# Two layers of attention-like convolution on one core: products moved to GpSimd, a bias product and a DMA moved, one stage of image 0 nested

## The chip, the cores and the metric

The kernel runs on one core of a Trainium2 chip. The core has TensorE (PE, matrix products, with its own row PEld for loading weights), VectorE (DVE), ScalarE (ACT), GpSimd (POOL) and SyncE (SP, here only a queue that issues DMAs). ScalarE and GpSimd issue DMAs too. The metric is the device time of one execution in microseconds, as the median over the runs.

## The reference

The input is 8 images of 512 channels and 32 x 32 = 1024 positions, all in float32. Layer 0 is attention with 8 heads of 64 channels, a projection and a residual; layer 1 is a product of two 1x1 convolutions without softmax, followed by a normalization over the whole batch.

```python
# layer 0
q, k, v = conv1x1(x, Wq, bq), conv1x1(x, Wk, bk), conv1x1(x, Wv, bv)   # as (B, 8, 64, 1024)
attn = softmax(einsum('bhdn,bhdm->bhnm', q, k) * 64 ** -0.5, axis=-1)
x = x + conv1x1(einsum('bhnm,bhdm->bhdn', attn, v), Wp, bp)
# layer 1
g, theta, phi = conv1x1(x, g_w, g_b), conv1x1(x, theta_w, theta_b), conv1x1(x, phi_w, phi_b)  # 256 channels
f = einsum('bcn,bdn->bcd', theta, phi) / 1024
z = conv1x1(einsum('bcd,bdn->bcn', f, g), W_w, W_b) + x
out = (z - mean(z)) * rsqrt(var(z) + 1e-5) * gamma + beta      # mean and var per channel over batch and positions
```

## The kernel before, in words

The images run one after the other. For each, PE works through stages: attention (scores, exponential on ScalarE, weighted sum of v), then the q, v and k of the *next* image, then the projection of the current image (`project`), theta and phi (`theta_phi`), g, the 256 x 256 product f, and z. Image 0's q, k and v come first of all, in the order q, k, v, and attention follows them directly; for later images the order is q, v, k, and the projection follows.

Large products are done by a Strassen-like scheme of seven smaller products instead of eight (`seven`). Some of the seven can be split once more in the same way (`nested`). The table `INNER` says which: with three of them nested, four remain plain (`FOUR`). Nesting needs sums of blocks of the data (`inner_sums`, `inner_parts`) and of the weights, both made on VectorE. The weights' sums are made once, in place, in `keep_inner`, and the result is copied to memory and reloaded for each later image. In the kernel before, image 0's q, k and v use seven plain products, since the inner sums of the weights aren't there yet, and `keep_inner` runs after each stage.

The products of a stage go to banks of PSUM, and the parts are read by ScalarE (the first contribution to an output block) and by VectorE (those added to it). A bank is used again when its readers are done. Banks have tags, and a list `free` passes them from stage to stage; `seven` reorders it at the end. Attention takes its first three score tiles from the first, second and fourth tag of that list.

The denominators of the softmax are sums over keys of the exponentials. VectorE adds the exponentials (`acc`, L456 and L458), and the accumulating DMAs from GpSimd's queue fold them (`together`, L488). For images 0 to 6, `all_denominators` (L518) is called inside the next image's q stage: 16 matmul records sum the folds, VectorE takes the reciprocal (L524), a DMA from ScalarE's queue writes it to memory (L526), and four DMAs from SyncE's queue read it back into a tile `r`, broadcast over the partitions (L569). Four products (L555, in `normalize`) then multiply the attention's output `o` by `r`. They are called at units 7, 8, 10 and 11 of the next image's v stage. The sums `t_o` over `o` for the projection are made during the k stage. In image 0, `bias_product` (L189) also runs there, after the denominators: it multiplies Wp by v's bias, so that the bias can be added after the projection; its weights were prepared during attention (`join_bias`).

The last image has no next image to fill its wait. Its denominators come in two halves (`denominators`, L532). The first is done during attention. The second is done during the g stage of image 6: reciprocal (L537), a DMA of 16 x 256 values from SyncE's queue (L541), and two broadcasts of 512 KB each (L550) for each half. The last four products and the projection follow.

The order on VectorE, PE and parts of SyncE's queue is the order of the program where an instruction is passed to `dve`, `pe` or `sp`. Otherwise a scheduler chooses it. The dictionaries `fills` hang small pieces of work behind numbered units of a stage. A unit is about one PSUM part of a product.

Of the kernel before, what the change touches and what calls it, by code (L numbers as in the profile page):

```python
# [8 lines left out]
F32 = mybir.dt.float32  # L9
I32 = mybir.dt.int32  # L10
AF = mybir.ActivationFunctionType
ALU = mybir.AluOpType
# [4 lines left out]
P = 128  # L17
# [13 lines left out]
def unshifted(ctx: ExitStack, tc: tile.TileContext, a: dict, out: bass.AP):  # L31
    nc = tc.nc
    B, C, H, W = a["x"].shape
    N = H * W
    CC = C // P
# [127 lines left out]
    def keep_inner(name, w):  # L163

        for n in range(len(INNER[name])):
            a11, a12, a22, a21, s2, s3, s4 = inner_blocks(w, name, n)
            for to, l, r, op in ((s3, a11, a21, ALU.subtract), (a21, a21, a22, ALU.add), (s2, a21, a11, ALU.subtract),
                                 (s4, a12, s2, ALU.subtract)):
                dve(nc.vector.tensor_tensor(to, l, r, op))
        wide = len(INNER[name]) * 3 * P  # L170
        kept[name] = dram.tile([P, 14 * w.shape[3] + wide], F32, tag=f"kept_{name}", name=f"kept_{name}")
        nc.sync.dma_start(kept[name][:, :14 * w.shape[3]], w.rearrange("p i k f -> p (i k f)"))
        nc.sync.dma_start(kept[name][:, 14 * w.shape[3]:], rest[name][:, :wide])
# [15 lines left out]
    def bias_product(t, ps):  # L189
        for oc in range(CC):  # L190
            pe(nc.tensor.matmul(ps[:, oc:oc + 1], t[:, oc * P:(oc + 1) * P], ones, start=True, stop=True,
                                skip_group_check=True))
        nc.vector.tensor_tensor(bp, bp, ps, ALU.add)
# [229 lines left out]
    def attention(b, q, k, v, near_end, make_f=None):  # L423
# [94 lines left out]
        def all_denominators(ps):  # L518

            t = folded.pop("t")  # L520
            den = ps[:, 0, :256]
# [6 lines left out]
            if b == 0:  # L528
                bias_product(t[:, 3, :], ps[:, 1, :CC])
            return d.rearrange("(j k x) m -> j k (x m)", j=2, k=2)  # L530

        def denominators(g, ps):  # L532
# [8 lines left out]
            nc.sync.dma_start(d, ri.rearrange("(x s) n -> x s n", s=8)[:, 0, :])  # L541
# [10 lines left out]
        def normalize(d):  # L552

            def product(at, of):
                dve(nc.vector.tensor_tensor(at, at, of, ALU.mult))  # L555
# [289 lines left out]
    data = {"11": b11, "21": b21, "22": b22, "t1": t[0], "t2": t[1], "t3": t[2], "t4": t[3]}  # L845
# [9 lines left out]
    k = heads_of(0, "k", w, bk, data, dve)  # L855
    keep_inner("WkT", w)
    load_w(nc.sync)
    w = weights("WvT")
    v = values(0, w, data)
    keep_inner("WvT", w)  # L860
    load_w(nc.sync)
    held = {}
    for b in range(B):
# [23 lines left out]
        if not last:  # L887
# [20 lines left out]
            else:  # L908
                w_p = loaded[1][1]
                for unit, which in ((12, (3, 4)), (14, (5, 6))):  # L910
                    fills[unit] = lambda which=which: weight_sums(w_p, corner["WpT"], which, dve)
# [277 lines left out]
```

## Time and profile before

| what | value |
|---|---|
| median of 3 runs | 2139.47 us (2138.54 to 2140.98) |
| the profiled execution, its own time | 2139.02 us |
| its span, first to last instruction | 2137.2 us |
| PE busy | 2111.9 us, 12982 matmul records |
| VectorE busy | 1411.3 us |
| ScalarE busy | 745.8 us |
| GpSimd busy | 144.9 us (189 DMA issues of 766 ns) |
| mean granted clock of PE | 0.995 |
| one image in the middle (attention to attention) | 261.5 us |

One float32 matmul appears as several records: a product of 128 x 128 weights with 512 columns takes 0.43 us of PE and shows as two. Records overlap: the mean duration in a group (593 ns for such a record) is longer than the distance between two starts. PE is busy nearly all the time, so the places where it waits matter, and with them the clock it is granted.

In lines of the timeline the first number is the start in us from the beginning of the span and the second the duration. Behind the engine come the line of the program, the operation and "output<-inputs". Square brackets hold idle time of the engine before it and what ended it. In a table of stretches each engine has its busy time and, in brackets, its number of instructions; the columns are length, PE, PEld, DVE, ACT, POOL, the granted clock (1.00 is full), the share of DMA time and GB/s.

### The profile page before, as it was taken

To read this page: it belongs to the slowest core of one execution; us is meant where nothing else is said; L and a number is where in the kernel's file an instruction comes from. 1 tells how busy PE (TensorE), PEld (TensorE's weight loads), DVE (VectorE), ACT (ScalarE), POOL (GpSimd) and SP (SyncE) were. 2 spreads that over 40 slices of the span, in tenths; PEclk is the share of its full clock that TensorE was granted. 3 is DMA by queue.
4 is the path that set the end of the run, shared out by engine and by line. 5 is a ranking of instruction groups with operands and counts; after the bars stand their busy time and mean duration, and the time that the engine had idled before them with its cause. 6 is when DMAs were issued, how large, how long until landed. Compare 5 with 4: busy or idle time off the path is not lost.

```text
span 2137.2 us, 31130 instructions
## 1 busy us (share of the span) xinstructions
PE 2111.9 (99%) x12982; PEld 1127.2 (53%) x12982; DVE 1411.3 (66%) x1855; ACT 745.8 (35%) x869; POOL 144.9 (7%) x193
## 2 busy tenths in 40 slices
PE   9999999999999999999999999999999999999996
PEld 4534764347733567335673366633766347643462
DVE  5466667676576675766757677676774676656746
ACT  1464103641046310463105631066212652056106
POOL 0011000110001100010001100011000110011000
PEclk9999999999999999999999999999999999999998
DMA  6522444225142241423324242242334224122758
GB/s 208 192 41 35 121 192 136 41 30 163 73 140 40 43 146 73 145 39 60 125 94 127 40 99 86 114 107 41 99 133 173 38 38 131 56 56 40 224 201 343
DMA packets 53318, 228.75 MB, mean 107 GB/s; under 512 B 10673, under 2 KB 17329, under 8 KB 45617
## 3 DMA queue, kind: packets, MB, share of 16 engines
q1 hardware_dynamic: 42272, 200.34, 27.2%
q0 software_dynamic: 9072, 24.78, 9.6%
q8 instruction: 104, 1.70, 0.3%
q10 hardware_dynamic: 1824, 1.55, 0.3%
q14 instruction: 46, 0.37, 0.1%
HBM read 146.23 MB, written 46.86 MB: 90 GB/s over the span
## 4 chain that ended last, share of the span: by engine, by line
PE 97%; ACT 1%; DVE 1%; DMA 1%; issue 0%; SPq 0%; DVEq 0%; ACTq 0%
PE ps L449 21%; PE po L475 21%; PE ptp L310 9%; PE pp L310 7%; PE pq L310 6%; PE pv L310 6%; PE pk L310 5%; PE pg L310 4%; PE pv_in_s L258 3%; PE pq_in_s L261 3%; PE pk_in_s L261 3%; PE pz L310 3%; PE pf L657 2%; PE pp_in_s L261 2%; PE pwf L712 1%; ACT z L832 1%
## 5 line engine op out<-in xcount | busy, mean ns | idle before, releaser
L452 ACT ACTIVATE e<-ps 128x1024 f32<-128x1024 f32 x512 | 522.3, 1023 | 429.1 <-PE ps L449 422.9
L458 DVE TENSOR_TENSOR acc<-acc,e 128x1024 f32<-128x1024 f32 x384 | 470.2, 1225 | 143.4 <-ACT e L452 140.0
L449 PE MATMUL ps<-q,k 64*64 64x512 f32 x4096 | 529.8, 590 | 0.0
L475 PE MATMUL po<-e,v 64*64 64x512 f32 x4096 | 529.0, 589 | 0.0
L475 PEld LDWEIGHTS po<-e,v 64*64 64x64 f32 x4096 | 156.7, 133 | 282.8 <-issue 275.3
L449 PEld LDWEIGHTS ps<-q,k 64*64 64x64 f32 x4096 | 155.4, 133 | 283.5 <-issue 274.5
L488 POOL DMA_DIRECT2D fold<-acc x189 | 144.7, 766 | 1837.3 <-PE ps L449 746.5
L700 ACT ACTIVATE g<-pg,gb 128x512 f32<-128x512 f32 x31 | 21.3, 687 | 476.4 <-PE pg L310 476.3
L456 DVE TENSOR_TENSOR acc<-e,e 128x1024 f32<-128x1024 f32 x64 | 78.4, 1225 | 133.9 <-ACT e L452 133.9
L310 PE MATMUL ptp<-w_tp,t_x 128*128 128x256 f32 x512 | 114.4, 380 | 0.0
L310 PEld LDWEIGHTS ptp<-w_tp,t_x 128*128 128x128 f32 x512 | 97.5, 190 | 13.0
L310 PE MATMUL pp<-t_o,w_WpT 128*128 128x512 f32 x208 | 100.9, 593 | 0.0
L310 PE MATMUL pv<-w_WvT,t_x 128*128 128x256 f32 x400 | 100.8, 380 | 0.0
L310 PE MATMUL pq<-t_x,w_WqT 128*128 128x512 f32 x200 | 100.6, 596 | 0.0
L310 PE MATMUL pk<-t_x,w_WkT 128*128 128x512 f32 x200 | 100.1, 593 | 0.0
L310 PE MATMUL ptp<-w_tp,x 128*128 128x256 f32 x384 | 86.8, 380 | 0.0
L420 DVE TENSOR_TENSOR v<-v,pv_in_s 128x256 f32<-128x256 f32 x119 | 49.8, 421 | 56.0 <-PE pv_in_s L258 39.5
L336 DVE TENSOR_TENSOR k<-k,pk_in_s 128x256 f32<-128x256 f32 x119 | 47.9, 420 | 48.9 <-PE pk_in_s L261 36.5
L310 PEld LDWEIGHTS ptp<-w_tp,x 128*128 128x128 f32 x384 | 73.1, 190 | 13.2 <-issue 3.8
L336 DVE TENSOR_TENSOR q<-q,pq_in_s 128x256 f32<-128x256 f32 x119 | 48.2, 417 | 46.4 <-PE pq_in_s L261 34.1
L310 PEld LDWEIGHTS pv<-w_WvT,t_x 128*128 128x128 f32 x400 | 69.7, 191 | 5.9
L310 PE MATMUL pp<-o,w_WpT 128*128 128x512 f32 x144 | 67.8, 593 | 1.9 <-DVE o L555 1.9
(198 smaller groups left out, 2305.6 us busy)
## 6 DMA issues: line engine op xcount, KB each, us to landing
fold<-acc POOLq DMA_DIRECT2D x189, 128.0 KB, 3.1
w_WqT<-kept_WqT SPq DMA_DIRECT2D x7, 2368.0 KB, 8.8
w_WvT<-kept_WvT SPq DMA_DIRECT2D x7, 2368.0 KB, 8.5
w_WkT<-kept_WkT SPq DMA_DIRECT2D x7, 2368.0 KB, 16.2
r<-den_d SPq DMA_DIRECT2D x32, 512.0 KB, 6.9
x<-in_x_dram SPq DMA_DIRECT2D x30, 512.0 KB, 5.9
w_WpT<-kept_WpT SPq DMA_DIRECT2D x6, 2176.0 KB, 8.2
w_tp<-kept_tp SPq DMA_DIRECT2D x7, 1792.0 KB, 7.4
```

The lines of the kernel that those rows point to most:

```text
L258: pe(nc.tensor.matmul(ps[:, i, :], d[di][:, i * P:(i + 1) * P], a[wi], start=s not in begun and not i, stop=True, skip_group_check=True))
L261: pe(nc.tensor.matmul(ps, a[wi], d[di], start=s not in begun, stop=True, skip_group_check=True))
L310: pe(nc.tensor.matmul(to_ps, lhsT(k), rhs(k), start=(s, at) not in begun, stop=(k == nk - 1), skip_group_check=True))
L336: pin(nc.vector.tensor_tensor(at, at, ps if len(ps.shape) == 3 else ps.unsqueeze(1), ALU.add))
L420: lambda q, ps: dve(nc.vector.tensor_tensor(at(q), at(q), as_v(ps), ALU.add)), **how)
L449: pe(nc.tensor.matmul(ps[c * P // 2:(c + 1) * P // 2, j, :], k[r, p, keys], q[r, p, h * 512:(h + 1) * 512], start=True, stop=True, skip_gr ...
L452: nc.scalar.activation(e, ps, AF.Exp, scale=SCALE)
L456: nc.vector.tensor_tensor(accs[u], es[u, 0], e, ALU.add)
L458: ins = nc.vector.tensor_tensor(accs[u], accs[u], e, ALU.add)
L475: pe(nc.tensor.matmul(ps[j * D:(j + 1) * D, r, :], v[keys, m, (2 * p + j) * D:(2 * p + j + 1) * D], e[keys, j, :], start=(m == 0), stop=(m ...
L488: nc.gpsimd.dma_start(to, part_of, accum_op=ALU.add)
L657: pe(nc.tensor.matmul(to, theta[l][:, i, :], phi[r][:, i, :], start=(i == 0), stop=(i == NB // 2 - 1), skip_group_check=True))
```

## The change

Five edits:

- The four products of `o` with `r` are issued on GpSimd instead of VectorE for images 0 to 6. The last image keeps VectorE.
- In image 0 `bias_product` comes before the matmuls of the denominators instead of after the reciprocal. Its result is copied out of PSUM by ScalarE first, and VectorE adds the copy.
- The last DMA of reciprocals (second half, last image) is issued from ScalarE's queue instead of SyncE's.
- Image 0's v uses the nested scheme with three nested products. For that the inner sums of the data are made in image 0's k stage, the inner sums of Wv before the v stage, and those of Wk during it, in three parts. The copies of the weights to memory change places accordingly.
- In image 0 the four sums for Wp are made one by one at units 8, 9, 12 and 13 of the k stage instead of two each at 12 and 14.

```diff
     def keep_inner(name, w):
         for n in range(len(INNER[name])):
-            a11, a12, a22, a21, s2, s3, s4 = inner_blocks(w, name, n)
-            for to, l, r, op in ((s3, a11, a21, ALU.subtract), (a21, a21, a22, ALU.add), (s2, a21, a11, ALU.subtract),
-                                 (s4, a12, s2, ALU.subtract)):
-                dve(nc.vector.tensor_tensor(to, l, r, op))
+            inner_weights(name, w, n)
+        keep_all(name, w)
+
+    def inner_weights(name, w, n):
+        a11, a12, a22, a21, s2, s3, s4 = inner_blocks(w, name, n)
+        for to, l, r, op in ((s3, a11, a21, ALU.subtract), (a21, a21, a22, ALU.add), (s2, a21, a11, ALU.subtract),
+                             (s4, a12, s2, ALU.subtract)):
+            dve(nc.vector.tensor_tensor(to, l, r, op))
+
+    def keep_all(name, w):
...
@@ bias_product
-        nc.vector.tensor_tensor(bp, bp, ps, ALU.add)
+        got = small.tile([P, CC], F32, tag="got", name="got")
+        nc.scalar.copy(got, ps)
+        nc.vector.tensor_tensor(bp, bp, got, ALU.add)
@@ all_denominators
             t = folded.pop("t")
+            if b == 0:
+                bias_product(t[:, 3, :], ps[:, 1, :CC])
             den = ps[:, 0, :256]
...
-            if b == 0:
-                bias_product(t[:, 3, :], ps[:, 1, :CC])
@@ denominators
-            nc.sync.dma_start(d, ri.rearrange("(x s) n -> x s n", s=8)[:, 0, :])
+            (nc.scalar if g else nc.sync).dma_start(d, ri.rearrange("(x s) n -> x s n", s=8)[:, 0, :])
@@ normalize
             def product(at, of):
-                dve(nc.vector.tensor_tensor(at, at, of, ALU.mult))
+                if make_f:
+                    dve(nc.vector.tensor_tensor(at, at, of, ALU.mult))
+                else:
+                    dve(nc.gpsimd.tensor_tensor(at, at, of, ALU.mult))
@@ image 0
-    data = {"11": b11, "21": b21, "22": b22, "t1": t[0], "t2": t[1], "t3": t[2], "t4": t[3]}
+    data = {"11": b11, "21": b21, "22": b22, "t1": t[0], "t2": t[1], "t3": t[2], "t4": t[3], "name": "x_0"}
...
-    k = heads_of(0, "k", w, bk, data, dve)
-    keep_inner("WkT", w)
+    k = heads_of(0, "k", w, bk, data, dve,
+                 fills={unit: lambda of=of: inner_sums(data, of, dve) for unit, of in ((8, "21"), (10, "22"), (12, "t4"))})
+    wk, w = w, weights("WvT")
+    keep_inner("WvT", w)
+    v = values(0, w, data, inner="WvT",
+               fills={unit: lambda n=n: inner_weights("WkT", wk, n) for n, unit in enumerate((9, 11, 13))})
+    keep_all("WkT", wk)
     load_w(nc.sync)
-    w = weights("WvT")
-    v = values(0, w, data)
-    keep_inner("WvT", w)
     load_w(nc.sync)
@@ fills of the next image's k, image 0 only
-                for unit, which in ((12, (3, 4)), (14, (5, 6))):
-                    fills[unit] = lambda which=which: weight_sums(w_p, corner["WpT"], which, dve)
+                for unit, which in ((8, 3), (9, 4), (12, 5), (13, 6)):
+                    fills[unit] = lambda which=which: weight_sums(w_p, corner["WpT"], (which,), dve)
```

`nc.gpsimd.tensor_tensor` is the same operation as on VectorE, and `nc.scalar.dma_start` the same DMA from another queue.

## The prediction

> **What bounds the kernel now.** I read the page's busy table first (TensorE, PE, busy 2111.9 of 2137.2 us, VectorE only 1411.3), then the waits of PE, then a table of stages. PE's busy time can hide a slow clock, so I also asked for the granted clock. The waits of PE alone; columns are microseconds in total, times, longest:
>
> ```profile
> PE den L191 <- DVE fold L524: 1.9, 1, 1.9
> PE pp L310 <- DVE o L555: 1.9, 1, 1.9
> PE warm_ps L357 <- DVE folds L367: 1.1, 1, 1.1
> PE pk_in_s L261 <- DVE k L336: 0.3, 1, 0.3
> ```
>
> That is all: four waits in 12982 matmuls. The other images run without a gap, so work taken off another engine there gains nothing. The stages (start:end, length, PE busy):
>
> ```profile
> 53.80:78.04 24.24, 24.24 (x113) 21.12 (x111) 6.68 (x15) 4.30 (x5) 0.00 (x0) 1.00 0.50 201
> 209.78:215.04 5.26, 3.38 (x29) 2.18 (x29) 2.34 (x3) 0.00 (x0) 0.00 (x0) 1.00 0.03 9
> 215.04:239.90 24.86, 24.86 (x149) 22.75 (x148) 15.05 (x24) 4.53 (x7) 0.00 (x0) 0.93 0.64 185
> 239.90:263.30 23.40, 23.07 (x76) 14.01 (x75) 16.17 (x27) 5.64 (x10) 0.00 (x0) 1.00 0.18 51
> 741.10:764.29 23.19, 23.19 (x150) 21.56 (x149) 15.37 (x25) 4.53 (x7) 0.00 (x0) 1.00 0.69 199
> 764.29:787.15 22.86, 22.86 (x77) 14.01 (x76) 15.67 (x28) 5.64 (x10) 0.00 (x0) 1.00 0.26 98
> ...
> 216.00:217.00 1.00, 1.00 (x4) 0.82 (x3) 1.00 (x2) 0.00 (x0) 0.00 (x0) 0.50 0.00 0
> ```
>
> Line 1 is image 0's v with seven plain products; line 5 is a later image's v, with nested products, 1.05 us shorter. Line 2 is the denominators and bias product of image 0, with 1.88 us in which PE stood still. Line 3 is the v stage behind them: the same work as line 5 but 1.67 us longer, because the clock (third number from the right) fell to half, as the last line shows. Lines 4 and 6 are the k stages: image 0 loses 0.5.
>
> The end of the last attention and the order on VectorE (DVE) inside a later image, from the timeline (start, duration) and the table of DMA issues (KB each, us to landing):
>
> ```profile
> 1997.81 0.51 SPq L541 DMA_DIRECT2D den_d<-ri  x1
> 2003.49 1.09 SPq L550 DMA_DIRECT2D r<-den_d  x2
> 2010.41 2.36 DVE L555 TENSOR_TENSOR o<-o,r 128x1024 f32<-128x1024 f32 x2 [3.38 <-DMA r<-den_d]
> den_d<-ri SPq DMA_DIRECT2D x1, 16.0 KB, 5.7
> den_d<-fold ACTq DMA_DIRECT2D x1, 32.0 KB, 1.7
> 759.18 1.22 DVE L555 TENSOR_TENSOR o<-o,r 128x1024 f32<-128x1024 f32 x1
> 764.46 0.42 DVE L420 TENSOR_TENSOR v<-v,pv_in_s 128x256 f32<-128x256 f32 x1 [0.89 <-PE pv_in_s L258]
> 764.79 2.35 DVE L420 TENSOR_TENSOR v<-v,pv 128x1024 f32<-128x1024 f32 x2
> 771.77 1.22 DVE L206 TENSOR_TENSOR t_o<-o 128x1024 f32<-128x1024 f32 x1
> ```
>
> **What the Trainium skill says.** "GPSIMD Engine Reference", section 3.1 (Elementwise), prices a two-input product of 2048 float32 columns at 4497 ns; no run here has one. The same page's section 8 (Key points) says GpSimd shares its SBUF interfaces with VectorE and contends with DVE instructions that have two SBUF inputs; untested here. "TensorE: Matmul & The Clock Gate", Part 1, says that a free-running window of 3413 ns with PE idle halves its clock: the trace agrees (0.50 from 214.9 to 218.3, one window). "DMA: Bandwidth & Descriptors", Queues, rings and completion order: SyncE and ScalarE own separate rings on the same 16 DMA engines, served in turn; the two landing times above, 5.7 behind other traffic and 1.7 alone, fit that but do not prove it.
>
> **The change part by part.** The profiled execution took 2139.02 us, of which 2137.2 is span; the median of the runs is 2139.47. I sum against the profiled one and carry the difference over.
>
> *Bias product ahead of the denominators (image 0).* Before, its eight matmul records waited 1.88 for the reciprocal. They now follow finished work and the denominators need no reciprocal, so the 1.88 goes. The bias matmuls (1.05) stay. PE is then never idle here, and later images show that the denominators alone leave the clock at 1.00, so the half-clock window should go too: 1.67. Bounds for the second: 0 (the window is free-running; the executions timed before need not all have been hit) to 1.67; I take 1.67. The added copy on ScalarE (nearest row: a 128x1 activation, 0.30) and DVE's 0.16 add lie ahead of the reciprocal, but the denominators need another 1.0 on PE, which covers both. The reciprocal itself comes about 1.0 later, and r with it. Sum: -3.55.
>
> *Image 0's v with three nested products.* PE: 24.24 becomes 23.19, -1.05. Preparation: twelve data sums on DVE (0.42 each, about 4.3 in sequence) fall into its 7.99 idle before 43.75. WvT's own sums are done at 48.5; twelve 128x128 sums (0.29 each) and two k additions follow, so they end near 54.6, and the first nested product comes after eight plain ones, at 57.2: 2.6 spare. WkT's twelve sums move into the v stage, four at a time (1.2), where the nested rhythm leaves DVE 0.89 idle per pair of additions. The end is worse. The plain v ended with a ScalarE copy, and the third score tile found its bank free. Now it reuses the bank that DVE empties last: in the later image the last pair of additions runs 764.79 to 767.14, 2.85 after PE's v ended at 764.29. The third tile is due after two of 0.86, that is at 1.72, and so waits 1.1; WkT's last four sums add 0.3. Nothing behind it absorbs this, PE being the bound in attention. Cost +1.4 (0 to 2), net +0.35. On SyncE's queue WvT's copy now precedes WkT's, and both reloads follow; the first is wanted at 188, the queue is through by about 84, ahead of the first fold at 91.8. Hidden.
>
> *WpT's sums spread over four places (image 0's k).* The two pairs of 0.69 delayed an addition and PE waited 0.33. One at a time they fit into DVE's idle stretches: the large k addition then stands where line 6's stage has it. -0.33. On the queue the 1792 KB copy of WpT now precedes three loads for theta and phi; alone such a copy lands in 5.7. The sums that read them have moved behind the second projection product, some 8 us in, about when the loads land; PE needs that bank 2 us later still. Zero, and up to 2 if this cover fails.
>
> *Products on GpSimd, images 0 to 6.* 28 products of 1.22 leave DVE (34 us), which PE never waited for there: gain 0. Cost of one by the page: about half of 4497 ns, an estimate of 2.25. The r tiles are issued 743.44 to 745.2 and land after 4.5 to 9.9, so the first half is there near 750 and the last at 755.1. Two products then end at 754.6 and two more at 759.6. The first reader is the sum at 771.77: 12 spare. The limit is (771.77 - 750)/4 = 5.4 per product. In those 9 us DVE does only v additions, with one input in PSUM, so the page's contention should not apply. GpSimd's next accumulating DMA comes in the next attention. An ISA instruction stands ahead of the first product; the page's section 2.1 has about 6 us for a first call, and GpSimd is idle from 200.4 until r lands near 225. Hence 0; above, the loss is the contention rival's below.
>
> *Last reciprocals by ScalarE's queue.* Before, the 16 KB write sat behind two 512 KB broadcasts of r and landed after 5.7, and the next broadcasts waited for it until 2003.49. ScalarE has nothing between 1994.3 and 2001.3. Landing in 1.7 to 4 us, the write lets them start at about 2000.5 (bounds 1999.6 and 2002.9). They still share the engines with the first pair, which moves data until 2002.1, and took 6.9 before; I expect landing near 2008. PE ran out of work at 2009.82 and resumed at 2011.68; it needs r by about 2008.5. Gain 1.86 at most, 0.6 at the late bound; I take 1.75.
>
> Sum: -3.55 + 0.35 - 0.33 + 0 - 1.75 = -5.28. 2139.02 - 5.3 = 2133.7 for a profiled execution, 2134.2 at the median.
>
> **Rivals.** *Contention.* GpSimd and DVE hold each other up although the additions read PSUM. The additions take 0.42 each, two per 1.755 us of PE; they become PE's bound when one takes more than 0.85. At 0.95 the loss is about 0.2 per 1.755, some 1 us per image over 9 us, 7 in all: 2141. If each product holds an addition for its whole 2.25, minus 0.89 slack, 28 of them cost 38: near 2172. For: the page says the interface is shared. Against: one SBUF input per addition.
>
> *The half clock stays, or was not typical.* The bias matmuls stream one column each; with the denominators they are 2 us of little array work. Then -1.67 fails: 2135.9. For: the cause of the dip is inferred from one case. Against: a 1.86 us stop near 2010 left the clock at 1.00.
>
> *The broadcasts were bandwidth-bound.* Moving the write then gains nothing, since the second pair only queues behind the first: 2136.0. For: DMA share near 1 from 1998 to 2002. Against: it is 0.11 and 0.00 in the two microseconds after.
>
> *No stall after image 0's v.* If the banks come free in time: 2132.8.
>
> **How the numbers follow.** 0.2%, about what a measurement of this kernel can tell from no change, is 4.28 us: the border lies at 2135.19. Forecast 0.60, own range 2132.5 to 2135.9, of which about 0.09 falls beyond the border; half clock 0.14 and bandwidth 0.12, both within 0.2%; no stall 0.05, faster; contention 0.09, nearly all slower. Faster 0.56, same 0.36, slower 0.08. The range 2131.8 to 2137.6 leaves out most of the contention and a tail on each side, where two small failures join.
>
> **What would show it.** PE's waits should lose the 1.9 on L524 and the 0.3; the clock should be 1.00 from 208 to 220. Image 0's v should be about 23.2, followed by a PE wait of 1 to 1.5 on DVE's v. GpSimd products should last about 2.25 and end before t_o; DVE's v additions should stay at 0.42. The last reciprocals should land in under 4 us and PE's wait on o shrink below 0.7. I am wrong if later images lengthen from 261.5 us, if products last over 5.4, or if PE waits in the nested v for weights.

## The result and the profile after

The changed kernel took 2135.07 us (median of 14 runs, 2133.99 to 2136.88). The kernel before, on the same chip, took 2139.22 (14 runs, 2138.39 to 2141.50). The ratio is 0.998 with a 95% interval of 0.9972 to 0.9988: 4.2 us less, with 2.6 to 6.0 in the interval. The profiled execution of the changed kernel took 2134.36 us, with a span of 2132.6, against 2137.2 before. In the changed kernel most lines of the code stand about ten lines lower: L310 is L320, L555 is L566 for VectorE and L568 for GpSimd.

The waits of PE in the changed kernel; the columns are microseconds in total, times, longest:

```profile
PE pp L320 <- DVE o L566: 1.6, 1, 1.6
PE warm_ps L367 <- DVE folds L377: 1.1, 1, 1.1
PE ps L459 <- DVE v L430: 1.0, 1, 1.0
PE den L525 <- ACT got L202: 0.3, 1, 0.3
```

The 1.9 behind the reciprocal of image 0 is gone and so is the 0.3 in the k stage. A new wait of 1.0 has come, on v, and the wait for o in the last image is nearly what it was. Now image 0's turn. The timeline of PE (start, duration) and the table of stretches for the v and the k stage behind it:

```profile
209.25 0.95 PE L199 MATMUL den<-ones,fold 128*128 128x1 f32 x8
210.45 1.07 PE L525 MATMUL den<-fold,folds 128*32 128x256 f32 x16 [0.25 <-ACT got L202]
```

```profile
212.90:236.10 23.20, 23.20 (x150) 21.55 (x149) 10.85 (x21) 4.53 (x7) 9.35 (x4) 1.00 0.69 200
236.10:258.90 22.80, 22.80 (x76) 14.05 (x76) 16.88 (x28) 5.65 (x10) 0.00 (x0) 1.00 0.17 52
```

The bias product (one column wide) now runs ahead of the denominators and waits for nothing; the denominators wait 0.25 for ScalarE's copy. The clock of the v stage is 1.00, not 0.93, and its 23.20 us are those of every later image. The k stage takes 22.80 instead of 23.40. The fifth pair of a row is GpSimd: in the v stage 9.35 us for the four products (x4).

The end of image 0's v, and the end of the last attention, from the timeline of PE, DVE and the two DMA queues:

```profile
76.36 1.95 PE L459 MATMUL ps<-q,k 64*64 64x512 f32 x16
76.92 2.34 DVE L430 TENSOR_TENSOR v<-v,pv 128x1024 f32<-128x1024 f32 x2
79.32 1.09 PE L459 MATMUL ps<-q,k 64*64 64x512 f32 x8 [1.01 <-DVE v L430]
...
1991.48 8.23 SPq L560 DMA_DIRECT2D r<-den_d  x4
1993.35 0.51 ACTq L551 DMA_DIRECT2D den_d<-ri  x1
2005.70 2.36 DVE L566 TENSOR_TENSOR o<-o,r 128x1024 f32<-128x1024 f32 x2 [3.54 <-DMA r<-den_d]
2006.98 3.70 PE L320 MATMUL pp<-o,w_WpT 128*128 128x512 f32 x8 [1.63 <-DVE o L566]
```

and the write of the last reciprocals in the table of DMA issues (KB, us to landing):

```profile
den_d<-ri ACTq DMA_DIRECT2D x1, 16.0 KB, 5.3
```

The third score tile starts when the last pair of additions to v (76.92 to 79.26) is over. The write of reciprocals is issued from ScalarE's queue, and it lands after 5.3 us, where SyncE's queue took 5.7.

To find where time went I cut every profile at the same places: the start of image 0's v, of the next q, of image 0's projection (pp), of the g stage of image 6, in which the last denominators are made (pg), of the last image's projection, and the end. A stage starts with its first record of PE in the timeline. The spans are given to a tenth, so the last column is good to about 0.05. Lengths in us:

| kernel | program start to v | v to next q | q to pp | pp to last pg | pg to pp | pp to end |
|---|---|---|---|---|---|---|
| before | 53.77 | 134.30 | 75.23 | 1723.17 | 19.75 | 130.98 |
| after | 53.08 | 134.55 | 71.21 | 1723.17 | 19.75 | 130.84 |

The stage from q to pp holds the bias product and Wp's sums: -4.02. The nested v with all that follows it costs +0.25. The long part in the middle, 1723.17 us of seven images, did not move by a hundredth. The start of the program, in which the two kernels do the same up to the k stage, was 0.69 shorter. It varied from 52.98 to 54.57 over all kernels of this study, whatever was edited, with PE waits of 0.3 to 1.0 us for the first weights or for k in some of them; I count it as scatter, and with it the single times below, which hold it too.

### The profile page after: what moved, and what is told of

Same layout as the page of the kernel before. It is cut to its first block, busy times and chain, and to the rows that moved or that the text cites. A ratio compares the mean times of both kernels' runs of the same rounds, so it can differ in the third digit from the quotient of the medians.

```text
span 2132.6 us, 31250 instructions
## 1 busy us (share of the span) xinstructions
PE 2108.4 (99%) x13018; PEld 1124.3 (53%) x13018; DVE 1390.1 (65%) x1856; ACT 747.5 (35%) x873; POOL 210.3 (10%) x221
## 4 chain that ended last, share of the span: by engine, by line
PE 97%; ACT 1%; DVE 1%; DMA 1%; issue 0%; SPq 0%; DVEq 0%; ACTq 0%
PE po L485 21%; PE ps L459 21%; PE ptp L320 9%; PE pp L320 7%; PE pq L320 6%; PE pk L320 6%; PE pv L320 5%; PE pg L320 4%; PE pv_in_s L268 3%; PE pk_in_s L271 3%; PE pq_in_s L271 3%; PE pz L320 3%; PE pf L670 2%; PE pp_in_s L271 2%; PE pwf L725 1%; ACT z L845 1%
## 5 line engine op out<-in xcount | busy, mean ns | idle before, releaser
L430 DVE TENSOR_TENSOR v<-v,pv_in_s 128x256 f32<-128x256 f32 x136 | 56.8, 421 | 97.6 <-PE pv_in_s L268 79.4
L320 PE MATMUL ptp<-w_tp,t_x 128*128 128x256 f32 x512 | 114.4, 379 | 0.0
L320 PEld LDWEIGHTS ptp<-w_tp,t_x 128*128 128x128 f32 x512 | 97.3, 190 | 13.2
L320 PE MATMUL pp<-t_o,w_WpT 128*128 128x512 f32 x208 | 100.8, 592 | 0.0
L320 PE MATMUL pq<-t_x,w_WqT 128*128 128x512 f32 x200 | 100.6, 596 | 0.0
L320 PE MATMUL pk<-t_x,w_WkT 128*128 128x512 f32 x200 | 100.0, 592 | 0.0
L320 PE MATMUL pv<-w_WvT,t_x 128*128 128x256 f32 x384 | 98.8, 380 | 0.0
L320 PE MATMUL ptp<-w_tp,x 128*128 128x256 f32 x384 | 86.8, 379 | 0.0
L568 POOL TENSOR_TENSOR o<-o,r 128x1024 f32<-128x1024 f32 x28 | 65.4, 2354 | 153.7 <-DMA r<-den_d 131.5
L320 PEld LDWEIGHTS ptp<-w_tp,x 128*128 128x128 f32 x384 | 73.0, 190 | 13.3 <-issue 3.8
L320 PE MATMUL pp<-o,w_WpT 128*128 128x512 f32 x144 | 67.8, 593 | 1.6 <-DVE o L566 1.6
```

What stands on the lines that cost most here:

```text
L320: pe(nc.tensor.matmul(to_ps, lhsT(k), rhs(k), start=(s, at) not in begun, stop=(k == nk - 1), skip_group_check=True))
L430: lambda q, ps: dve(nc.vector.tensor_tensor(at(q), at(q), as_v(ps), ALU.add)), **how)
L568: dve(nc.gpsimd.tensor_tensor(at, at, of, ALU.mult))
```

## The experiments

My theory after this: the gain is the bias product's place and Wp's sums, the products on GpSimd are worth nothing, the nested v is a small loss, and ScalarE's queue is worth some 0.2, since the write is held by the broadcasts queued ahead of it. Most effects are smaller than a few tenths of a per cent, so each edit is judged by its stage in the table's cut, not by the whole time.

### The products back on VectorE

```diff
-                if make_f:
-                    dve(nc.vector.tensor_tensor(at, at, of, ALU.mult))
-                else:
-                    dve(nc.gpsimd.tensor_tensor(at, at, of, ALU.mult))
+                dve(nc.vector.tensor_tensor(at, at, of, ALU.mult))
```

> The changed kernel with the 28 products of o with r back on VectorE; all else kept. Theory: TensorE never waited for VectorE in the steady images, so the seven images from image 0's projection on keep their 1723.1 us, the whole run stays within 0.5 us of the changed kernel's, and VectorE's busy time rises by 28 x (1.22 - 0) = 34 us less what the inner sums of image 0 changed. Rival (relief of VectorE is part of the gain): the steady part grows by 1 us or more, or a wait of TensorE on VectorE appears among those four.

Measured: pp to last pg 1723.18 against 1723.17, and every other stage of image 0 unchanged to 0.01; 2135.64 us as a whole, against 2134.36 in the profiled run of the changed kernel; the start of the program (54.03) accounts for 0.95 of that and the tail for 0.35. VectorE's busy time rose from 1390.1 to 1421.4 us. The theory holds: 28 products moved from one engine to another and TensorE did not notice. The time is 1.3 higher, more than the 0.5 expected, all of it outside the part that the edit touches.

### Image 0's bias product back behind the reciprocal

```diff
-            if b == 0:
-                bias_product(t[:, 3, :], ps[:, 1, :CC])
             den = ps[:, 0, :256]
...
+            if b == 0:
+                bias_product(t[:, 3, :], ps[:, 1, :CC])
             return d.rearrange("(j k x) m -> j k (x m)", j=2, k=2)
```

(and the direct addition out of PSUM, without ScalarE's copy.)

> The changed kernel with image 0's bias product back behind the reciprocal, added straight out of PSUM; all else kept. Theory: TensorE waits 1.9 us again for the reciprocal, and a window of half clock follows in the v stage behind it, so that q start to projection start of image 0's turn grows from 71.30 to about 74.9 (+3.6), with the v stage at about 24.9 instead of 23.20. Rival (the half clock depended on where the free-running window fell): the stage grows by 1.9 only, to 73.2, the v stage stays at 23.2 and the clock at 1.00. Rival (the gain came from the spread sums of Wp alone): no growth.

The timeline of PE in this kernel, and the stretches behind it, whose third number from the right is the clock:

```profile
213.16 1.34 PE L199 MATMUL den<-ones,fold 128*128 128x1 f32 x8 [1.88 <-DVE fold L532]
214.35 2.06 PE L318 MATMUL pq<-t_x,w_WqT 128*128 128x512 f32 x2
216.20 1.06 PE L269 MATMUL pq_in_s<-i_x,w_WqT 128*128 128x256 f32 x2
```

```profile
214.00:215.00 1.00, 1.00 (x4) 0.83 (x4) 0.16 (x1) 0.00 (x0) 0.00 (x0) 0.50 0.10 33
215.00:216.00 1.00, 1.00 (x2) 0.34 (x1) 0.00 (x0) 0.00 (x0) 0.00 (x0) 0.50 0.00 0
```

The stop of 1.88 is back, and with it the half clock: the two records of one product, which take 1.02 at full clock, took 2.06. (The 0.43 us given further up for a product of 512 columns is the time of one of its two records; 56 records of 0.43 make up image 0's 28 products of k.) From q to pp it is 74.63 instead of 71.21: +3.42. The stop is 1.88 of it; the rest, 1.54, is the slow window (3.41 us at half clock, so at most 1.71) less the 0.25 for which the changed kernel waits for ScalarE's copy, and small differences. The window fell on the end of the q stage, not on v as I expected: it began 0.61 us after the stop's end, in the kernel before 2.25 us after it. So the half clock follows this stop, but not at a fixed distance. The two rivals (1.9 only, or nothing) fall. The whole run took 2140.90; 2.2 of its distance from the changed kernel lie in the tail, which is taken up below.

### The same edit alone, on the kernel before

The edit of the change (bias product first, ScalarE's copy) put into the kernel before, and nothing else.

> The kernel before with the earlier bias product as its only edit. Theory (this edit is nearly the whole gain): from the start of q to the start of image 0's projection 75.23 becomes 71.8 (-3.4: the stop of 1.88 and the slow window behind it), and the median falls by 3 to 3.8 us. Rival (the half-clock window was chance and is now hit elsewhere as often): the stage gains 1.9 and the median 2 or less.

Measured: q to pp 71.81 instead of 75.23, -3.42, the same to a hundredth as when it is undone. The median was 2136.17 (15 runs) against 2140.37 (20 runs), ratio 0.9982 with an interval of 0.9974 to 0.9989. The median fell by 4.2, a little more than expected, inside its interval (2.4 to 5.6). So far as these medians can tell, one edit of five gives what the whole change gives; by the stages it gives 3.42 of about 3.9.

### Wp's sums in pairs again

```diff
-                for unit, which in ((8, 3), (9, 4), (12, 5), (13, 6)):
-                    fills[unit] = lambda which=which: weight_sums(w_p, corner["WpT"], (which,), dve)
+                for unit, which in ((12, (3, 4)), (14, (5, 6))):
+                    fills[unit] = lambda which=which: weight_sums(w_p, corner["WpT"], which, dve)
```

> The changed kernel with the four sums for Wp two and two at units 12 and 14 of image 0's k stage again; all else kept. Theory (the spread is worth what that stage lost before): the k stage grows from 22.80 to 23.40 us and TensorE's wait of 0.3 on k is back. Rival (the stage got shorter for another reason, such as the products leaving VectorE): 22.80 stays.

Measured: the k stage 23.40 and PE's wait of 0.3 on k back, as the theory has it: this edit is worth 0.60, not only the wait of 0.33. The part from pp to the last pg also took 0.33 longer here (1723.50), all of it in image 4's k stage, for which I have no reason. With a tail of 132.7 the whole run took 2137.87.

### Image 0's v with plain products again

```diff
-    k = heads_of(0, "k", w, bk, data, dve,
-                 fills={unit: lambda of=of: inner_sums(data, of, dve) for unit, of in ((8, "21"), (10, "22"), (12, "t4"))})
-    wk, w = w, weights("WvT")
-    keep_inner("WvT", w)
-    v = values(0, w, data, inner="WvT",
-               fills={unit: lambda n=n: inner_weights("WkT", wk, n) for n, unit in enumerate((9, 11, 13))})
-    keep_all("WkT", wk)
+    k = heads_of(0, "k", w, bk, data, dve)
+    keep_inner("WkT", w)
     load_w(nc.sync)
+    w = weights("WvT")
+    v = values(0, w, data)
+    keep_inner("WvT", w)
     load_w(nc.sync)
```

> The changed kernel with image 0's v back to seven plain products and the weights' inner sums after them; all else kept. Theory: v itself grows from 23.1 to 24.2 us, the wait of 1.0 us of the third score tile goes, and from the start of v to the start of the next q 134.46 becomes 134.2 (-0.26): the nested v is a small loss. Rival (the nested v is worth its 1.05 us and the wait would be there anyway): 135.5.

Measured: v to next q 134.30 instead of 134.55, the wait for v gone: -0.25, as the theory says. Yet the whole run took 2137.48, 3.1 more than the profiled run of the changed kernel. 1.1 of that is the start of the program, and 2.25 is the tail. Its stretches around the last projection show why:

```profile
2006.00:2007.00 1.00, 0.21 (x1) 0.00 (x0) 0.00 (x0) 0.00 (x0) 0.00 (x0) 1.00 0.74 272
2007.00:2008.00 1.00, 0.00 (x0) 0.00 (x0) 0.78 (x1) 0.00 (x0) 0.00 (x0) 1.00 0.98 416
2008.00:2009.00 1.00, 0.50 (x1) 0.50 (x2) 1.00 (x2) 0.00 (x0) 0.00 (x0) 0.76 1.01 430
2009.00:2010.00 1.00, 1.00 (x2) 0.34 (x2) 0.96 (x2) 0.00 (x0) 0.00 (x0) 0.50 0.81 344
```

and PE's timeline there:

```profile
2008.50 5.38 PE L320 MATMUL pp<-o,w_WpT 128*128 128x512 f32 x8 [2.30 <-DVE o L566]
```

The stop for o, 2.30 us here, was followed by a window of half clock, and eight records that took 3.70 in the changed kernel took 5.38. The same stop stands in eleven of the profiles, with 1.6 to 2.3 us. Five had the window: 2.30, 2.3, 2.17, 2.06 and 1.9 us (this kernel, the bias edit alone, the bias product undone, SyncE's queue, Wp in pairs), with 132.7 to 133.1 from pp to the end. Six had not: 2.13, 2.05, 1.86, 1.8, 1.65 and 1.63 us (two of them before and after), with 130.8 to 131.4. So the window is neither tied to an edit nor to the length of the stop alone.

What tells the five from the six is where the stop fell. In each of the fourteen traces every later change of the clock comes a whole number of steps of 3.413 us after the first one, to within 0.001 of a step. On this grid a stop lies inside one step or is cut by a border. Two stops of the same length, each line one step of the grid (second number: PE busy; third from the right: clock). Lines 1 and 2 are the kernel with the write on SyncE's queue, lines 3 to 5 the one with the products on VectorE:

```profile
2005.12:2008.53 3.41, 1.35 (x4) 0.48 (x3) 1.57 (x2) 0.00 (x0) 0.00 (x0) 1.00 0.98 351
2008.53:2011.95 3.42, 3.42 (x5) 1.35 (x5) 3.39 (x4) 0.00 (x0) 0.00 (x0) 0.50 0.97 401
2003.75:2007.17 3.42, 2.56 (x6) 0.77 (x5) 0.10 (x1) 0.00 (x0) 0.00 (x0) 1.00 0.97 252
2007.17:2010.58 3.41, 2.23 (x5) 1.06 (x6) 3.38 (x3) 0.00 (x0) 0.00 (x0) 1.00 0.99 417
2010.58:2013.99 3.41, 3.41 (x9) 1.52 (x8) 3.41 (x5) 0.00 (x0) 0.00 (x0) 1.00 1.04 413
```

The stop of 2.06 lay inside one step, and the next step ran at half clock. The stop of 2.05 was cut into 0.86 and 1.19, and the clock stayed full. It is so in all eleven: the five with a window had all of their 1.91 to 2.30 us in one step; the six without had at most 1.63 in one step. "TensorE: Matmul & The Clock Gate", Part 1, of the Trainium skill says that the window is free-running, so that its position differs from run to run; the traces agree: the first change, from which the grid is counted, lies between 4.07 and 6.95 us from the start of the span. A single time of this kernel carries 2 us of it.

### The banks at the end of image 0's v

```diff
     keep_all("WkT", wk)
+    free[:] = [free[0], free[1], free[3], free[2]]
     load_w(nc.sync)
```

> The changed kernel with the last two PSUM banks exchanged between image 0's v and its attention: the third score tile takes the bank that the last nested product left, and the first output sums, one step of 0.86 us later, take the bank that VectorE empties last. Theory (the 1.01 us wait is for the bank that VectorE empties with its last pair of additions): the wait falls to 0.1 to 0.3, and from the start of v to the start of the next q 134.46 becomes about 133.6. Rival (the additions are late as a whole, so that the other bank is late too): the wait stays at 0.7 or more.

The waits of PE in this kernel:

```profile
PE pp L320 <- DVE o L566: 1.7, 1, 1.7
PE po L485 <- DVE v L430: 0.2, 1, 0.2
```

(The two others, on folds and on ScalarE's copy, are as in the changed kernel.) The wait of 1.0 became one of 0.2, one step later; v to next q 133.78, -0.77, a little less than the 0.9 expected; the run took 2133.73. The wait was for that one bank. With this line the nested v is a gain of 0.52 on plain products instead of a loss.

### The write of the last reciprocals

Three runs take the write apart. On SyncE's queue again, behind the broadcasts:

```diff
-            (nc.scalar if g else nc.sync).dma_start(d, ri.rearrange("(x s) n -> x s n", s=8)[:, 0, :])
+            nc.sync.dma_start(d, ri.rearrange("(x s) n -> x s n", s=8)[:, 0, :])
```

> The changed kernel with the last write of reciprocals back on SyncE's queue, behind the two broadcasts, as before the change; all else kept. Theory: landing 5.7 instead of 5.3, the end of the last attention to the projection 25.1 instead of 24.9, whole run +0.2. Rival (the queue is worth the 1.75 that was forecast, and the profile of the changed kernel was an unlucky one): +1 or more.

On SyncE's queue, ahead of the first half's broadcasts:

```diff
+            sp(nc.sync.dma_start(d, ri.rearrange("(x s) n -> x s n", s=8)[:, 0, :]))
             if g:
                 rows_of(0, first_den)
             d = dram.tile(...)
-            (nc.scalar if g else nc.sync).dma_start(d, ri.rearrange("(x s) n -> x s n", s=8)[:, 0, :])
```

(the line that makes `d` moves up with the write.)

> The changed kernel with the last 16 KB write of reciprocals on SyncE's queue again, but put ahead of the two broadcasts of the first half's r, which so start only when the reciprocal is ready (about 1993.4 instead of 1991.5). Theory (the write was late because the first pair of broadcasts, 1 MB, was already queued on the same DMA engines): it lands after about 2 us instead of 5.3, the second pair follows the first without a pause, r is whole some 1 to 1.5 us earlier after the reciprocal (about 11 instead of 12.4), and TensorE's wait for o falls from 1.63 to 0.2 to 0.6. Rival (the write of 16 rows of 1 KB out of every eighth partition is slow by itself): it still takes 5 us, the second pair starts as late as before and everything is about 2 us later.

On ScalarE's queue, with the first half's r in memory of its own, a free part of a weights tile, broadcast long before:

```diff
-            if g:
-                rows_of(0, first_den)
...
-            rows[g] = rows["all"][:, 4 * g:4 * g + 4, :].rearrange("q i n -> q (i n)")
+            rows[g] = foldp.tile([P, 2048], F32, tag="fold", name=f"r_{b}") if g else rest["WgT"][:, 512:2560]
...
+            if make_f and i == 50:
+                rows_of(0, first_den)
```

(`normalize` then reads the two halves from their two places.)

> The changed kernel with the first half's r in memory of its own (a free part of the weights tile), broadcast in the middle of the last attention, where nothing waits for it; the write of the second half on ScalarE's queue then has no broadcast ahead of it. Theory (queued broadcasts delay the write): it lands after 1.7 to 2.2 us, the second pair of broadcasts follows at once and takes 5 to 6.5, r is whole near 8.5 us after the reciprocal instead of 12.4, and TensorE's wait of 1.63 for o goes, so that the whole run is 1.6 us shorter. Rival (slow by itself): the landing stays at 5 us, and r comes at 11 to 12.

Measured, with r complete where the second pair of products starts, counted from the start of the last reciprocal (the expectations count from its end, 1.75 later, so their 11, 8.5 and 12.4 are 12.8, 10.3 and 14.1 here):

| write | landing, us | r complete, us | PE's wait for o | pp to end |
|---|---|---|---|---|
| ScalarE's queue, behind the broadcasts (8 profiles) | 5.2 to 5.8 | 14.13 to 14.80, mean 14.46 | 1.6 to 2.3 | 130.8 to 133.1 |
| SyncE's queue, behind them (before, this undo, bias alone) | 5.4 to 5.7 | 14.38, 14.57, 14.76 | 1.9, 2.1, 2.3 | 131.0 to 133.0 |
| SyncE's queue, ahead of them | 1.7 | 14.56 | 1.1 | 130.3 |
| ScalarE's queue, first half early (this kernel, and with the banks exchanged) | 1.7 | 10.61, 10.98 | none | 128.9 |

The DMA table of the kernel with the write first, and the timeline of SyncE's queue and DVE:

```profile
den_d<-ri SPq DMA_DIRECT2D x1, 16.0 KB, 1.7
```

```profile
1995.48 2.39 SPq L560 DMA_DIRECT2D r<-den_d  x4
2002.78 2.36 DVE L566 TENSOR_TENSOR o<-o,r 128x1024 f32<-128x1024 f32 x2 [5.58 <-DMA r<-den_d]
2007.54 2.36 DVE L566 TENSOR_TENSOR o<-o,r 128x1024 f32<-128x1024 f32 x2 [1.15 <-DMA r<-den_d]
```

The same two views of the kernel with the first half early:

```profile
den_d<-ri ACTq DMA_DIRECT2D x1, 16.0 KB, 1.7
w_WgT<-den_d SPq DMA_DIRECT2D x2, 512.0 KB, 5.7
```

```profile
1997.17 2.35 DVE L562 TENSOR_TENSOR o<-o,w_WgT 128x1024 f32<-128x1024 f32 x2
2003.65 2.36 DVE L562 TENSOR_TENSOR o<-o,r 128x1024 f32<-128x1024 f32 x2 [2.87 <-DMA r<-den_d]
```

Three things follow. The write is not slow by itself: with no broadcast ahead it lands in 1.7 us from either queue. Behind two broadcasts of 512 KB it lands only about when these are done, from either queue: ScalarE's own queue bought about 0.1 us, within the scatter.

The trace's DMA packets show where the time went: in the changed kernel the write's sixteen pieces of 1 KB took about 0.1 us each, but the first started at 1997.22, 3.9 us after the issue, when all 128 pieces of the two broadcasts had started; with no broadcast ahead the first started 1.2 us after the issue.

And an early landing was not enough. With the write first, four broadcasts run without a pause and take 12.1 us from their issue to the last products (14.2 in the changed kernel), but they start 2.6 us later after the reciprocal, so r is whole no sooner: my expectation of 11 us was wrong here. PE's wait of 1.1 looks better than it is, since PE also lost 0.77 to "issue" just ahead of the projection, and from pg to the end this kernel took 0.4 more than the changed one. A write that lands early while the first pair of broadcasts starts no later was not tried. Only moving the first megabyte out of this place took the stop away: about 1.9 us less from pp to the end than in the changed kernel, of which 1.63 was the stop. The single time of that run, 2134.01, was only 0.35 lower, because its program start happened to be 1.5 longer (54.57 to v).

The whole run with the write back on SyncE's queue took 2137.24, 2.9 more than the profiled run of the changed kernel, which would be the rival's "+1 or more"; but 0.84 of that is the start of the program and 2.06 the tail, where its stop fell inside one step of the clock's grid.

### More work on GpSimd, beside other work of VectorE

The products met only additions with one input in PSUM. What would others have met? Four more products per attention, images 1 to 6, read by nothing:

```diff
+            if 0 < b < B - 1 and i == 20:
+                extra = block(f"extra_{b}").rearrange("p h n -> p (h n)")
+                for _ in range(4):
+                    nc.gpsimd.tensor_tensor(extra, q[:, 0, :], k[:, 0, :], ALU.mult)
```

> The changed kernel with four more GpSimd products of 128x1024 in the attention of each image from 1 to 6, their result read by nothing, at a place where VectorE adds tiles of e with both inputs in SBUF (1.22 us each, one per 1.75 us of TensorE). It measures the contention that the products of the change might have met. Theory (GpSimd holds up only VectorE work with two SBUF inputs, and there is 0.5 us of slack per addition): GpSimd's own products stay near 2.35, VectorE's additions grow, to between 1.3 and 2.4 us, while they run together, and the 24 extra products cost TensorE 0 to 3 us in the whole. Rival (no contention at all): additions stay at 1.22 to 1.24 and nothing moves. Rival (each product holds an addition for its whole length): additions reach 3.5 and TensorE waits by some 1 us per product, 10 to 25 us in the whole.

DVE's and GpSimd's timeline in image 2's attention, in this kernel:

```profile
641.06 1.23 DVE L468 TENSOR_TENSOR acc<-acc,e 128x1024 f32<-128x1024 f32 x1 [0.49 <-ACT e L462]
641.68 12.75 POOL L599 TENSOR_TENSOR extra<-q,k 128x1024 f32<-128x1024 f32 x4
642.78 6.12 DVE L468 TENSOR_TENSOR acc<-acc,e 128x1024 f32<-128x1024 f32 x2 [0.50 <-ACT e L462]
648.82 3.39 DVE L466 TENSOR_TENSOR acc<-e,e 128x1024 f32<-128x1024 f32 x1
662.90 1.23 DVE L466 TENSOR_TENSOR acc<-e,e 128x1024 f32<-128x1024 f32 x1 [0.74 <-ACT e L462]
```

An addition of two SBUF tiles, 1.23 us alone, took 3.1 to 3.4 here beside GpSimd (2.8 to 3.4 over the six images), about as long as one of its products, and four products took 12.75, 3.2 each instead of 2.35. That is the mechanism of the strong rival; my own guess was 1.3 to 2.4 and no effect on GpSimd. Its price of 10 to 25 us was too high: the whole run took 2143.13, and TensorE lost 7.5 us in the seven images (1730.65), 6.1 of it in six waits for ScalarE, which in turn waited six times, 18.8 us in all, for the buffer that the extra result held. To see whether the buffer or the late additions were to blame, the extra result was sent to an unused quarter of the fold tile:

```diff
-                extra = block(f"extra_{b}").rearrange("p h n -> p (h n)")
                 for _ in range(4):
-                    nc.gpsimd.tensor_tensor(extra, q[:, 0, :], k[:, 0, :], ALU.mult)
+                    nc.gpsimd.tensor_tensor(folded["t"][:, 3, :], q[:, 0, :], k[:, 0, :], ALU.mult)
```

> As the run with four extra GpSimd products in each attention of images 1 to 6, but their unread result goes to an unused quarter of the fold tile instead of to one of the ten buffers that e is made in. There the additions beside them took 2.8 to 3.4 us instead of 1.22 and TensorE lost 7.5 us in all, in waits for ScalarE, which waited for the buffer. Theory (the contention is real, but TensorE's loss came through the occupied buffer, since the late additions catch up later): additions again reach 2.8 to 3.4 us, and the seven images from image 0's projection on take 1723 to 1724 us. Rival (the late additions hold so many e tiles that ScalarE runs out of buffers anyway): TensorE still loses 3 to 7 us.

It did not answer that, and I leave it open. These extra instructions were given no fixed place in GpSimd's order (the products of the change have one), and without the buffer the scheduler put them earlier, to the border of the k stage and the projection. The time was 2176.45, with 1764.78 us in the seven images, 41.6 more. DVE's, GpSimd's and PE's timeline there, in image 2's turn:

```profile
791.28 0.42 DVE L228 TENSOR_TENSOR i_o<-o 128x256 f32<-128x256 f32 x1
791.59 9.74 POOL L598 TENSOR_TENSOR fold<-q,k 128x1024 f32<-128x1024 f32 x4 [26.89 <-issue]
791.62 2.59 DVE L228 TENSOR_TENSOR i_o<-o,i_o 128x256 f32<-128x256 f32 x1
794.13 0.41 DVE L346 TENSOR_TENSOR k<-k,pk_in_s 128x256 f32<-128x256 f32 x1
794.46 2.34 DVE L346 TENSOR_TENSOR k<-k,pk 128x1024 f32<-128x1024 f32 x2
796.72 2.41 DVE L228 TENSOR_TENSOR i_t_o<-t_o 128x256 f32<-128x256 f32 x1
799.17 2.44 DVE L228 TENSOR_TENSOR i_t_o<-t_o,i_t_o 128x256 f32<-128x256 f32 x1
803.98 1.22 PE L271 MATMUL pp_in_s<-i_o,w_WpT 128*128 128x256 f32 x2 [5.32 <-DVE x L346]
```

and the first of PE's waits:

```profile
PE pp_in_s L271 <- DVE x L346: 26.6, 5, 5.3
```

This is the clearest view of the contention. Sums of two SBUF tiles of 256 columns (i_o, i_t_o) take 0.42 us alone and 2.4 to 2.6 beside GpSimd: each is held for about one product. GpSimd's own products kept 2.34 to 2.43 beside these short sums. The additions between them that read PSUM (k) take 0.41 and 1.17 as always, while the same products run. TensorE stopped 5.3 us five times (26.6). Each time the clock then stood at half for two steps of the grid, 6.83 us, in this view from 802.8 to 809.6, the first 1.2 us of it still in the stop. TensorE was busy for 27.6 us of these five stretches, so that they cost about 13.8 of the other 15.

### The change with two more edits

The bank order and the early first half together, on the changed kernel.

> The changed kernel with the two further edits that gained in their own runs: the last two PSUM banks exchanged between image 0's v and its attention, and the first half's r of the last image broadcast early into memory of its own. Theory (both act at different places and add up): v to next q 133.78 instead of 134.55, the last projection to the end about 128.9 instead of 130.8 to 133.1, because TensorE neither waits for o nor risks a slow window behind that wait; median about 2131.8, that is 3 us under the changed kernel and 7 under the kernel before, ratio about 0.9966. Rival (the early broadcasts disturb the folds of the last attention in some executions): gain of the bank order only, 2134.3.

PE's waits are down to three, of 1.1 (on folds), 0.3 (on ScalarE's copy) and 0.2 (on v). v to next q 133.78, pp to end 128.90: the two add up. The median was 2131.97 (5 runs, 2131.59 to 2133.22) against 2140.37 of the kernel before (20 runs), ratio 0.9966 with an interval of 0.9952 to 0.998: 8.4 us, where the change gave 4.2 against another set of runs. The changed kernel itself was not timed in this comparison.

## Why the prediction was right, and where not

The forecast was 2134.2, in a range of 2131.8 to 2137.6, and the median came to 2135.07, at the border (2135.19) between faster and what can't be told from no change; the ratio, 0.998, lies on it too. By steps:

| step of the sum | predicted | measured | by |
|---|---|---|---|
| bias product ahead | -3.55 | -3.42 | undone, and alone |
| image 0's v nested | +0.35 | +0.25 | undone |
| Wp's sums spread | -0.33 | -0.60 | undone |
| products on GpSimd | 0 | 0.0 | undone |
| last reciprocals by ScalarE's queue | -1.75 | about -0.1 | undone, and eight profiles |
| sum | -5.28 | -3.9 | |

*The bias product.* Both of its parts were right: the stop of 1.88 and the slow window behind it. One term was put at nothing and was not: ScalarE's copy was to be covered by the denominators' work on PE, but the denominators themselves waited 0.25 for it. The bound of 0 for the window, which the rival "the half clock stays" took, was not met where this stop stood (two of two profiles), but the argument against it was weak. I had taken the stop of 1.86 near 2010 as one that leaves the clock alone; it was cut by a border of the grid, into 0.58 and 1.28, and in five of eleven profiles a stop at that place cost a window. I also said that the trace agrees with a window that has PE idle. It agrees in length only (3.41): at this stop and at the five near the end, the window ahead of the half clock had PE idle for part of it, 1.16 to 2.30 us. In the kernel before, just 1.16 of image 0's stop fell into the step ahead of the half clock, and 0.91 of the one-column bias product with it. That the clock fell all the same, where 1.63 of pure idle did not do it near 2005, suggests that such columns count as little work; this was not tested.

*The nested v.* The mechanism was right: the third score tile waits for the bank that VectorE empties last, which the exchange of banks shows. PE needed 23.28 us instead of 24.27, and the tile started 2.96 us after the end of v instead of 1.72, so 1.24 later (the profile shows 1.01 of it as a wait), where 1.1 was forecast for the bank and 0.3 for WkT's last sums. Of the 0.3 little is seen: VectorE's last additions ended 2.90 after PE's v, against 2.85 in the later image.

*Wp's sums.* The step counted only the wait that the profile shows, 0.33, while the stage itself said 0.5 over a later image. The stage lost 0.60 in all, and the edit gave all of it back. Mis-sized by 0.27.

*The products on GpSimd.* The zero was right and so, nearly, was the estimate of one product, half of the page's price for an addition of 2048 columns: 2.25 against 2.35 measured. The reason given, that the additions beside them read PSUM, is what the two runs with extra products show: one SBUF input is left alone, two are not. "GPSIMD Engine Reference", section 8 (Key points), of the Trainium skill says that GpSimd contends with VectorE instructions of two SBUF inputs; the runs agree, with 0.42 become 2.4 to 2.6 and 1.23 become 2.8 to 3.4. The rival of contention was thus right in its mechanism (each instruction held for a whole product) and wrong in the place, which the change avoids.

*The last reciprocals.* This is the step that failed: "Landing in 1.7 to 4 us, the write lets them start at about 2000.5". It landed after 5.2 to 5.8 us. The view had the two numbers, 5.7 behind other traffic and 1.7 alone, and I put the difference down to the queue where it is the traffic. "DMA: Bandwidth & Descriptors", Queues, rings and completion order, of the Trainium skill says that each DMA engine serves the rings in turn, a whole packet at a time; I had taken from that that a write in a ring of its own passes the broadcasts. The measurement decides: it did not pass them. Why the engines served it last is not shown. The rival "the broadcasts were bandwidth-bound" said that the move gains nothing, and this was so, but not for its reason. It let the write land early and the second pair queue behind the first; the write did not land early, and the pause that it caused cost about 2 us (14.2 us for the four broadcasts and their landing, 12.1 without a pause). Its price, 2136.0, is 0.9 over the result; Wp's sums (0.27) cover part of that, and the rest is inside the interval of the ratio.

The forecast time was therefore held by the first step, and in part by luck. The failed step left 1.65 ungained; Wp's sums gave 0.27 more than forecast, the others came about as forecast, and scatter did the rest: the medians differ by 4.15, the parts add up to 3.9.

## What to carry to other kernels

Where one engine is the bound, look for the few places in which it stops: here one stop of 1.88 us behind a reciprocal cost 3.4 with the slow window after it, and a stop can be turned away by running the work that is ready ahead of the work that waits. A stop that costs a slow window in one execution may not in the next, so judge a tail by more than one profile. A small transfer behind large ones was not saved by another queue here; taking the large ones out of its way in time did it. Work given to GpSimd was free where VectorE beside it read PSUM and held up VectorE's sums of two SBUF tiles, so see which of VectorE's instructions stand at that place, and fix the place.

## What the runs showed of the hardware

- A VectorE sum of two SBUF tiles waits for about one GpSimd product, however short it is itself: 256 columns 0.42 to 2.4 and 2.6 us, 1024 columns 1.23 to between 2.8 and 3.4. Additions with one input in PSUM keep 0.41 and 1.17 in the same microseconds.
- The clock changed only on a grid of 3.413 us, whose position differs from execution to execution. Of eleven stops of TensorE at one place, the five with 1.91 to 2.30 us of idle time in one step of the grid were followed by one step at half clock, the six with at most 1.63 in one step were not, though one of these lasted 2.13 in all. Five stops of 5.3 us brought two steps (6.83 us) at half clock each.
- A 16 KB write landed after 1.7 us alone and after 5.2 to 5.8 behind 1 MB of broadcasts, from its own queue as well as from theirs.
